# Position products of a self-attention block: eight array tiles of 64 rows and 32 columns for four of 128 rows and 64 columns

## The chip, the cores and the metric

The kernel runs on one core of a Trainium2 chip. A core has TensorE (matrix products, written PE in the profile, with its weight loads as PEld), VectorE (DVE), ScalarE (ACT), GpSimd (POOL) and SyncE (SP), and DMA engines that move data between DRAM and the on-chip memory. Products arrive in PSUM, from which ScalarE or VectorE read them. The metric is the device time in microseconds of one execution: 2402.37 us, the median of three runs (2398.63 to 2405.48). The profiled execution took 2397.5 us.

## The reference

Two bottleneck layers on 16 images of 1024 channels and 32 x 32 pixels, all in fp32. The first has local self-attention over a 3 x 3 window, with 32 heads of 8 channels; the second is an ordinary bottleneck with a 3 x 3 convolution. Cut to what matters here:

```python
q = relu(bn(conv1x1(x, wq)))                    # 256 channels: 32 heads of 8
k = relu(bn(conv1x1(x, wk)))
v = bn(conv1x1(x, wv))
pos = (pos_h + pos_w).reshape(1, c, 9, 1, 1)    # one value per channel and tap
kp = (unfold3x3(k) + pos).reshape(b, HEADS, 8, 9, h, w)
attn = softmax(einsum('bgdhw,bgdkhw->bgkhw', q, kp), axis=taps)
out = einsum('bgdkhw,bgkhw->bgdhw', unfold3x3(v), attn)
```

The logits split into q times the unfolded k, and q times `pos`. The second part is a product over the 8 channels of a head that is the same for every pixel, so TensorE can do it with a block matrix. Because the softmax ignores what all nine taps share, and `pos` is a sum of a part by row and a part by column, four values per head and pixel are enough (`NPOS = 4`: two row offsets and two column offsets against the third). These are the position products: 32 heads x 4 = 128 values for each of 1024 pixels of an image.

## The kernel before

The work is cut into stages by a list in the source: for each image a first 1x1 convolution (C), the projections q and k with the position products (Q), the projection v (V); then a fused stage (F) of the layer's last convolution and the next layer's first one; for each four images a 3x3 convolution in Winograd form (W); and the last 1x1 convolutions (U). The order of all instructions on each engine is written out ahead of time, in the schedule mode where the program's order is kept. A planner, the class `Side`, decides where VectorE's work (attention of an image, transforms for Winograd) is put among the TensorE stages; it counts with fixed costs, and the change does not touch those. The program builds the same sequence on TensorE, VectorE and ScalarE before and after, but for the position products.

`project(b)` makes q, k and v of one image. Its parts come in this order: k of the first 128 channels, q of both halves of the channels, k of the second 128 channels, then `positions()`, then v of both halves. Each convolution takes a tile of PSUM (`ps`, four in all, each of 1024 columns, which is two banks of 512), and ScalarE takes it out again: `norm` at L481 writes q, or writes k and v into `kp`, a padded buffer in the on-chip memory that k and v share. From `kp` each half goes to DRAM through SyncE's queue (L493), so v of a half may be written only once the store of k from there has landed.

`positions()` multiplies `pos`, a table of 128 channels by 64 columns for each half `n` of the channels (16 heads x 4 offsets, and zeros where the channel is not of the head), with q. It makes four matmuls: for each half of the pixels (512 columns) and each `n`, all 128 channels in, 64 values out. The output of `n` = 0 is on partitions 0 to 63 of `ps`, of `n` = 1 on 64 to 127. Seen from the array, these are two column tiles, each of 128 rows and 64 columns. ScalarE copies `ps` into `by_offset` (L515), and two DMAs on GpSimd's queue (L520) store it to DRAM in the order that attention wants: `by_quarter` gives a room of [quarter of the pixels, `n`, 64 values, 256 pixels]. From there it comes back as `pc` (L561), and VectorE adds it to the logits (L602, L605).

`by_offset` has one of three buffers in `zpool`, which transforms and Winograd results on VectorE and ScalarE share. GpSimd's queue is in order, and carries also the stores of q (L526), the loads for attention (L561) and most loads of inputs and stores of results (L345, L433). `fetch_attended` and `finish_attended` (L676 to L693) bring an attended image back from DRAM and apply a ReLU on ScalarE (L690) before the fused stage uses it (L405). VectorE's exp step is two ScalarE instructions (L628), which have a fixed place in ScalarE's order.

Of the kernel before, what the change touches and what calls it, by code (L numbers as in the profile page):

```python
# [13 lines left out]
P = 128  # L14
# [4 lines left out]
NW = WID // P  # L19
# [7 lines left out]
NJ = 4  # L27
JROWS = H // NJ
JPIX = JROWS * W
PW = W + 2  # L30
HALO = (JROWS + 2) * PW
NPOS = 4
FIRST = 4
G = P // HEAD_DIM
# [38 lines left out]
def sa_bottleneck_kernel(ctx: ExitStack, tc: tile.TileContext, x, w1t, wqkvt, w3t, u1t, u2t, u3t, params, out):  # L73
    nc = tc.nc
# [59 lines left out]
    def done_with(key):  # L134

        if last_use[key] == now[0]:
            more_weights()
# [3 lines left out]
    def col(name, j, n=1):  # L141
        return par[:, _COL[name] + j : _COL[name] + j + n]
# [42 lines left out]
    pos = const.tile([P, NW, G, NPOS], F32, tag="pos", name="pos")  # L185
# [117 lines left out]
    def inside(t, n):  # L303
        return t[:, n, 1 : 1 + H, 1 : 1 + W]

    def rows(ap):
        return ap.rearrange("p (r w) -> p r w", w=W)

    def halves(half):
        return slice(half * HALF, (half + 1) * HALF)  # L310
# [53 lines left out]
    def piece(name, half):  # L364
        return name, owner[now[0], name, half], half
# [87 lines left out]
    def by_quarter(name, b, width, per):  # L453


        t = dram.tile([NJ, NW, P * per // HEAD_DIM, width], F32, tag=f"{name}{b}", name=name)
        return t.rearrange("j n c w -> n c j w"), t.rearrange("j n (g d) w -> (j n g) (d w)", d=per)

    def project(b):

        h = hidden.pop(b)

        def conv(which, n):
            ps = psum.tile([P, HW], F32, tag="ps", name="ps")
            name, at = ("wqk", which * WID) if which < 2 else ("wv", 0)
            key, at = piece(name, 0), at + n * P
            for m in range(NW):
                for half in range(2):
                    nc.tensor.matmul(  # L469
                        ps[:, halves(half)],  # L470
                        pieces[key][:, m, at : at + P],
                        h[:, m, halves(half)],
                        start=(m == 0),
                        stop=(m == NW - 1),
                    )
            if n == NW - 1 and which:
                done_with(key)
            return ps

        def norm(dst, src, name, n, func):  # L480
            nc.scalar.activation(  # L481
                dst, src, func,
                bias=col(f"L0_conv_{name}_b", n), scale=col(f"L0_conv_{name}_s", n),
            )

        def halo(name, which, func):

            room, backs[name] = by_quarter(name, b, HALO, HEAD_DIM)
            for n in range(NW):
                norm(inside(kp, n), rows(conv(which, n)), name, n, func)  # L490

                block = kp[:, n]
                nc.sync.dma_start(  # L493
                    room[n], AP(block.tensor, block.offset, [block.ap[0], [JROWS * PW, NJ], [1, HALO]])
                )
                yield CHUNK

        backs = relaid[b] = {}
        q = hpool.tile([P, NW, HW], F32, tag="h", name=f"q_{b}")
        room, backs["q"] = by_quarter("q", b, JPIX, HEAD_DIM)  # L500

        def positions():

            ps = psum.tile([P, HW], F32, tag="ps", name="ps")
            for half in range(2):
                for n in range(NW):
                    nc.tensor.matmul(  # L507
                        ps[n * G * NPOS : (n + 1) * G * NPOS, halves(half)],
                        pos[:, n].rearrange("p g t -> p (g t)"),
                        q[:, n, halves(half)],  # L510
                        start=True,
                        stop=True,
                    )
            by_offset = zpool.tile([P, HW], F32, tag="z", name="by_offset")
            nc.scalar.activation(by_offset, ps, AF.Identity)  # L515

            room, backs["pos"] = by_quarter("pos", b, JPIX, NPOS)
            by_offset = by_offset.rearrange("p (j w) -> p j w", j=NJ)
            for n in range(NW):
                nc.gpsimd.dma_start(room[n], by_offset[n * G * NPOS : (n + 1) * G * NPOS])  # L520

        k = halo("bnk", 1, RELU)
        yield next(k)
        for n in range(NW):
            norm(q[:, n, :], conv(0, n), "bnq", n, RELU)
            nc.gpsimd.dma_start(room[n], q[:, n, :].rearrange("p (j w) -> p j w", j=NJ))  # L526
            yield CHUNK
        yield next(k)
        positions()
        side.add(b)  # L530
        written.add(("qk", b))
        relay("qk", b)
        yield 2.5
        for n, cost in enumerate(halo("bnv", 2, AF.Identity)):
            if n:
                written.add(("v", b))
                relay("v", b)
            yield cost
# [11 lines left out]
    def relay(what, b):  # L550

        if not ((what, b) in written and (what, b) in room_for):
            return
        moved, backs = projected.setdefault(b, {}), relaid[b]
        if what == "qk":
            shapes = (("q", "qc", [HEAD_DIM, JPIX]), ("bnk", "bnk", [HEAD_DIM, HALO]), ("pos", "pc", [NPOS, JPIX]))
        else:
            shapes = (("bnv", "bnv", [HEAD_DIM, HALO]),)
        def move(name, tag, shape):
            t = apool.tile([P] + shape, F32, tag=tag, name=f"{tag}_{b}")  # L560
            nc.gpsimd.dma_start(t.rearrange("p d w -> p (d w)"), backs[name])  # L561
            moved[name] = t.rearrange("p d (r w) -> p d r w", w=PW) if shape[1] == HALO else t
            if len(moved) in (3, 4):
                come[what, b] = max(side.vector, side.tensor) if b else side.tensor

        for i, shape in enumerate(shapes):
            if b < 2 or i == 0:
                move(*shape)
            else:

                moves.append((side.tensor + GAP * i, lambda shape=shape: move(*shape)))
# [841 lines left out]
```

## Time and profile before

| | busy us | share of 2397.5 us | instructions |
|---|---|---|---|
| PE matmuls | 2365.3 | 99% | 6112 |
| PE weight loads | 1143.9 | 48% | 6112 |
| VectorE | 2163.7 | 90% | 1783 |
| ScalarE | 935.0 | 39% | 891 |
| GpSimd | 465.8 | 19% | 853 |

The position matmuls are 128 records (two for each fp32 matmul, four matmuls for each of 16 images), from 50.0 to 1907.6 us. Their first starts lie near 50, 103, 153, 203, 311, 422, 472, 577, 682, 822, 1174, 1224, 1364, 1607, 1766 and 1906 us. The copy at L515 runs 16 times at 1.02 us, the stores at L520 32 times with 0.63 us of issue each, and land 6.4 us later in the median.

In the profile a line such as `L507 PE MATMUL ps<-q,pos` names the source line, the engine, the operation and what it writes and reads. A wait line names who waited and for what, then the us in all, the number of waits and the longest. In a timeline the first number is the start in us, the second the time until the last of the merged instructions ended, and brackets hold the idle time before it and what ended it. An engine that is busy 99% may still run below its peak, since matmuls overlap; how far apart they start says more than how long one lasts.

### The profile page before, as it was taken

To read this page: it belongs to the slowest core of one execution; us is meant where nothing else is said; L and a number is where in the kernel's file an instruction comes from. 1 tells how busy PE (TensorE), PEld (TensorE's weight loads), DVE (VectorE), ACT (ScalarE), POOL (GpSimd) and SP (SyncE) were. 2 spreads that over 40 slices of the span, in tenths; PEclk is the share of its full clock that TensorE was granted. 3 is DMA by queue.
4 is the path that set the end of the run, shared out by engine and by line. 5 is a ranking of instruction groups with operands and counts; after the bars stand their busy time and mean duration, and the time that the engine had idled before them with its cause. 6 is when DMAs were issued, how large, how long until landed. Compare 5 with 4: busy or idle time off the path is not lost.

```text
span 2397.5 us, 18521 instructions
## 1 busy us (share of the span) xinstructions
PE 2365.3 (99%) x6112; PEld 1143.9 (48%) x6112; DVE 2163.7 (90%) x1783; ACT 935.0 (39%) x891; POOL 465.8 (19%) x853
## 2 busy tenths in 40 slices
PE   8999999999999999999999999999999999999998
PEld 3444444444466444444466444444466444444843
DVE  4799998999999999998999999999989999875687
ACT  3323242233222574433122574334222553344278
POOL 3111111111111232111111232111111221111222
PEclk9999999999999999999999999999999999999999
DMA  9969686887798998686888998688788896788977
GB/s 358 350 229 313 241 280 227 258 302 250 287 318 264 322 394 317 225 265 222 260 308 290 306 396 304 233 277 282 251 301 301 308 353 223 255 281 268 331 285 294
DMA packets 295999, 691.05 MB, mean 288 GB/s; under 512 B 20064, under 2 KB 166496, under 8 KB 287456
## 3 DMA queue, kind: packets, MB, share of 16 engines
q0 software_dynamic: 118880, 470.87, 54.4%
q1 hardware_dynamic: 175648, 214.49, 28.3%
q10 hardware_dynamic: 1376, 4.51, 0.5%
q8 instruction: 49, 0.80, 0.1%
q14 instruction: 46, 0.38, 0.0%
HBM read 416.09 MB, written 273.70 MB: 288 GB/s over the span
## 4 chain that ended last, share of the span: by engine, by line
PE 92%; DVE 3%; DMA 3%; ACT 1%; issue 1%; ACTq 0%; SPq 0%; DVEq 0%
PE ps L373 36%; PE ps L405 29%; PE ps L469 13%; PE ps L786 9%; PE ps L1219 4%; PE ps L507 1%; DVE acc L646 1%; DVE acc L664 1%; DMA a<-a 1%; DMA bnk<-kp 1%; DMA U<-uw 0%; DMA uw<-u 0%; DMA V__2_8221<-v 0%; DMA v<-v 0%; DVE form L715 0%
## 5 line engine op out<-in xcount | busy, mean ns | idle before, releaser
L405 PE MATMUL ps<-a,w 128*128 128x512 f32 x1024 | 459.6, 594 | 4.3 <-ACT a L690 4.3
L373 PE MATMUL ps<-result,u 128*128 128x512 f32 x1024 | 459.8, 594 | 3.8 <-ACT result L432 3.8
L373 PE MATMUL ps<-x,w 128*128 128x512 f32 x1024 | 444.4, 595 | 6.4 <-DMA x<-in_x_dram 6.4
L646 DVE TENSOR_TENSOR acc<-e,bnv 128x2048 f32<-128x2048 f32 x144 | 327.6, 2283 | 33.6 <-ACT e L628 30.5
L405 PE MATMUL ps<-y,u 128*128 128x512 f32 x768 | 331.1, 592 | 0.0
L589 DVE TENSOR_TENSOR prod<-qc,bnk 128x2048 f32<-128x2048 f32 x144 | 324.0, 2287 | 1.7
L432 ACT ACTIVATE result<-ps,par 128x1024 f32<-128x1024 f32 x128 | 142.6, 1114 | 463.8 <-PE ps L405 395.4
L373 PEld LDWEIGHTS ps<-x,w 128*128 128x128 f32 x1024 | 195.4, 191 | 252.1 <-issue 251.9
L405 PEld LDWEIGHTS ps<-a,w 128*128 128x128 f32 x1024 | 194.8, 191 | 251.2 <-issue 242.5
L373 PEld LDWEIGHTS ps<-result,u 128*128 128x128 f32 x1024 | 194.8, 190 | 250.7 <-issue 238.2
L664 DVE TENSOR_TENSOR acc<-acc 128x2048 f32<-128x2048 f32 x128 | 293.4, 2292 | 4.4
L405 PEld LDWEIGHTS ps<-y,u 128*128 128x128 f32 x768 | 145.9, 190 | 183.3 <-issue 181.5
L469 PE MATMUL ps<-h,wqk 128*128 128x512 f32 x512 | 222.3, 592 | 0.0
L433 POOL DMA_DIRECT2D r<-result x128 | 68.8, 538 | 633.4 <-ACT result L432 618.0
L594 DVE TENSOR_TENSOR prod<-prod 128x2048 f32<-128x2048 f32 (+1 forms) x80 | 166.2, 2078 | 2.5
L469 PEld LDWEIGHTS ps<-h,wqk 128*128 128x128 f32 x512 | 97.2, 190 | 122.6 <-issue 110.0
L1052 ACT ACTIVATE h<-ps,par 128x1024 f32<-128x1024 f32 x32 | 38.6, 1205 | 280.6 <-PE ps L373 280.6
L432 ACT ACTIVATE result<-ps,bn_sh 128x1024 f32<-128x1024 f32 x96 | 106.6, 1112 | 102.5 <-PE ps L405 102.1
L481 ACT ACTIVATE kp<-ps,par 128x1024 f32<-128x1024 f32 x64 | 77.4, 1210 | 156.5 <-PE ps L469 114.6
L396 ACT ACTIVATE ps<-s 128x1024 f32<-128x1024 f32 x128 | 131.2, 1025 | 2.5
L345 POOL DMA_DIRECT2D x<-in_x_dram x120 | 63.8, 532 | 300.5 <-PE ps L373 229.3
L809 ACT ACTIVATE z<-ps 128x1024 f32<-128x1024 f32 x48 | 49.2, 1025 | 178.1 <-PE ps L786 130.4
(375 smaller groups left out, 2671.4 us busy)
## 6 DMA issues: line engine op xcount, KB each, us to landing
s<-in_x_dram POOLq DMA_DIRECT2D x128, 512.0 KB, 6.2
r<-result POOLq DMA_DIRECT2D x128, 512.0 KB, 4.1
out_dram<-result POOLq DMA_DIRECT2D x126, 512.0 KB, 6.4
x<-in_x_dram POOLq DMA_DIRECT2D x120, 512.0 KB, 5.1
r<-r POOLq DMA_DIRECT2D x111, 512.0 KB, 7.1
v<-v SPq DMA_DIRECT2D x96, 408.0 KB, 4.9
U<-uw SPq DMA_DIRECT2D x72, 512.0 KB, 4.1
bnk<-kp SPq DMA_DIRECT2D x32, 680.0 KB, 7.4
```

What stands on the lines that cost most here:

```text
L373: nc.tensor.matmul(ps[n][:, halves(half)], wt[:, c % (NC // 2), n * P : (n + 1) * P], src[:, halves(half)], start=(c == first), stop=(c == ...
L396: nc.scalar.activation(ps, loaded.pop((self.kind, self.b, o)), AF.Identity)
L405: nc.tensor.matmul(self.ahead[o][:, halves(half)], pieces[key][:, n, o % (NC // 2) * P :][:, :P], self.src[:, n, halves(half)], start=Fals ...
L432: nc.scalar.activation(to_, ps, RELU, bias=self.shift(o), scale=1.0)
L469: nc.tensor.matmul(ps[:, halves(half)], pieces[key][:, m, at : at + P], h[:, m, halves(half)], start=(m == 0), stop=(m == NW - 1),)
L481: nc.scalar.activation(dst, src, func, bias=col(f"L0_conv_{name}_b", n), scale=col(f"L0_conv_{name}_s", n),)
L589: nc.vector.tensor_tensor(by_row(t[:, two]), by_row(qc), kc[:, :, i : i + JROWS, j : j + W], ALU.mult)
L594: nc.vector.tensor_add(u[:, :, 0:4], u[:, :, 0:4], u[:, :, 4:8])
L646: nc.vector.tensor_tensor(by_row(dst), rows(e[:, k, :]).unsqueeze(1).to_broadcast([P, HEAD_DIM, JROWS, W]), vc[:, :, i : i + JROWS, j : j ...
L664: nc.vector.tensor_add(acc, acc, t)
L786: nc.tensor.matmul(acc[i][:, at, :, n, :], pieces[key][:, m, at, n * P : (n + 1) * P], v[:, at, :, m * (TILES + TR) :][:, :, :TILES], star ...
L1219: nc.tensor.matmul(ps, w, by, start=i in (1, 2, 7) and not (i == 2 and self.end), stop=True, skip_group_check=True)
```

## The change

Each position matmul is cut in two along the rows. The 16 heads of a half `n` belong to 128 channels; heads 0 to 7 use only channels 0 to 63, heads 8 to 15 only channels 64 to 127, and the rest of `pos` is zeros. So a matmul of 64 rows (channels) and 32 columns (8 heads x 4) holds all that is not zero. There are eight of them, for two row halves, two halves of the pixels and two `n`. `quadrant` chooses the 32 partitions of the output so that each of the eight has an array tile of its own, and so that two tiles that share columns of the array write different banks of PSUM. The aim is that all eight run at once in the array, in the place of two at once.

The price is that the outputs of the second half of the pixels lie in another order of partitions: the two groups of 32 in each `n` are swapped. The copy out of PSUM stays one instruction. The stores become five: one of 128 partitions for the first half of the pixels, whose order is the natural one, and four of 32 partitions for the second.

```diff
-            for half in range(2):
-                for n in range(NW):
-                    nc.tensor.matmul(
-                        ps[n * G * NPOS : (n + 1) * G * NPOS, halves(half)],
-                        pos[:, n].rearrange("p g t -> p (g t)"),
-                        q[:, n, halves(half)],
-                        start=True,
-                        stop=True,
-                    )
+
+            def quadrant(n, row, half):
+                return (2 * n + (row ^ half)) * P // 4
+
+            for row in range(2):
+                part, heads = slice(row * P // 2, (row + 1) * P // 2), slice(row * G // 2, (row + 1) * G // 2)
+                for half in range(2):
+                    for n in range(NW):
+                        to = quadrant(n, row, half)
+                        nc.tensor.matmul(
+                            ps[to : to + P // 4, halves(half)],
+                            pos[part, n, heads].rearrange("p g t -> p (g t)"),
+                            q[part, n, halves(half)],
+                            start=True,
+                            stop=True,
+                        )
             by_offset = zpool.tile([P, HW], F32, tag="z", name="by_offset")
             nc.scalar.activation(by_offset, ps, AF.Identity)
...
+            nc.gpsimd.dma_start(
+                AP(room.tensor, room.offset, [[JPIX, P], [P * JPIX, NJ // 2], [1, JPIX]]), by_offset[:, : NJ // 2]
+            )
             for n in range(NW):
-                nc.gpsimd.dma_start(room[n], by_offset[n * G * NPOS : (n + 1) * G * NPOS])
+                for row in range(2):
+                    at = quadrant(n, row, 1)
+                    nc.gpsimd.dma_start(
+                        room[n][row * P // 4 :][: P // 4, NJ // 2 :], by_offset[at : at + P // 4, NJ // 2 :]
+                    )
```

## The prediction

> **What bounds the kernel now.** I read the busy times first, then the waits of TensorE, then the order in time round one position product, then the chain of waits.
>
> ```profile
> PE 2365.3 (99%) x6112; PEld 1143.9 (48%) x6112; DVE 2163.7 (90%) x1783; ACT 935.0 (39%) x891; POOL 465.8 (19%) x853
> ...
> PE ps L405 <- ACT a L690: 4.3, 2, 2.9
> PE ps L373 <- ACT result L432: 3.8, 1, 3.8
> ...
> PE ps L469 <- ACT by_offset L515: 2.2, 1, 2.2
> ```
>
> TensorE (PE) is busy 99% of 2397.5 us, and its waits (us in all, times, longest) are single events: one at the start, one at 208 us (L469), one at 326 us (L373, for a result), the rest near the end (L405, for the attended image 15). Between 331 and 2121 us it never waits. So TensorE time taken out there comes off the end, unless VectorE (DVE, 90%) is so close behind that it becomes the bound.
>
> The timelines of the weight loads and of the matmuls near 311 us (image 4) show what a position product costs (start, duration, engine, line):
>
> ```profile
> 310.40 0.59 PE L469 MATMUL ps<-h,wqk 128*128 128x512 f32 x1
> 310.92 0.65 PE L507 MATMUL ps<-q,pos 128*64 128x512 f32 x2
> ...
> 310.92 0.20 PEld L507 LDWEIGHTS ps<-q,pos 128*64 128x64 f32 x4 [0.76 <-issue]
> 311.40 0.14 PEld L507 LDWEIGHTS ps<-q,pos 128*64 128x64 f32 x2 [0.29 <-issue]
> 311.83 0.14 PEld L507 LDWEIGHTS ps<-q,pos 128*64 128x64 f32 x2 [0.29 <-issue]
> 312.79 0.30 PEld L469 LDWEIGHTS ps<-h,wv 128*128 128x128 f32 x2 [0.81 <-issue]
> 313.32 0.19 PEld L469 LDWEIGHTS ps<-h,wv 128*128 128x128 f32 x1 [0.24 <-issue]
> 313.75 0.19 PEld L469 LDWEIGHTS ps<-h,wv 128*128 128x128 f32 x1 [0.24 <-issue]
> ```
>
> Each fp32 matmul of the program is two records, two passes. Full-width passes start 0.43 us apart (313.32, 313.75). The eight records of the four position matmuls start in pairs, at 310.92, 311.40, 311.83 and 312.3: the two column tiles already run beside each other. From the last full-width start before (310.40) to the first regular one after (313.32) is 2.92 us; without the block it would be 2 x 0.43 = 0.86. The block costs 2.06 us: four slots of 0.43 (1.72), and 0.34 at its two ends, where the array changes its tiling.
>
> **What the Trainium skill says.** "TensorEngine Tiling (Array Packing)", section Key Properties: different tiles load weights and multiply in parallel, and a change of tiling mode drains TensorE. The trace agrees on both: the pairs above, and the 0.34 us. "TensorE: Matmul & The Clock Gate", section Part 3, gives 10.6 times for 16 tiles of 32 x 32 and a span of one matmul plus about 4 ns for each further tile; the trace has only two tiles at once, and no row tiles. "PSUM — Partial Sum Buffer", section on bank collisions, says that row tiles must not write one bank and quadrant at once; here the XOR in `quadrant` sends the two row halves of one column strip to different banks. Nothing in the trace tests it.
>
> **The change, part by part.**
>
> *Matmuls.* Four of 128 rows and 64 columns go, eight of 64 rows and 32 columns come, still 512 columns of q each, so a pass should still take 0.43 us. Each of the eight has a tile of its own. If all start together, the block has two slots (first and second passes): 0.86 + 0.34 + 7 x 0.004 (the page's price of a tile, an estimate) = 1.23 us. Saved: 0.83 us an image. Upper bound 0.86 (no stagger), lower bound 0.72, if the first load and change cost a further 0.1. Sixteen images give 13.3 us at most.
>
> *Where it is lost.* Images 0 to 3 come before the wait at 208 us. Two lines of the chain there, after which TensorE goes on at 210.81:
>
> ```profile
> 208.67 1.19 ACT kp L481
> 209.85 0.91 ACT by_offset L515
> ```
>
> ScalarE reads image 3's positions at 209.85 because it stood at L690 until 207.5, waiting for the attended image 0 (a<-a), which VectorE ended at 189 and DMA brought. None of this hangs on TensorE; TensorE would come 4 x 0.83 = 3.3 us earlier and wait 3.3 us longer. Image 4 comes before the wait at 326 us, which ends with a kp store issued at 316.01 behind VectorE's v stores on the same queue and landing 12.23 us later; VectorE had no wait on TensorE there, so I count 0.83 as lost too. Images 5 to 15 (position products at 422 to 1906 us) keep theirs: 11 x 0.83 = 9.1 us.
>
> *Whether VectorE keeps up.* Only the attention of image 15 is late in the chain. Its waits on TensorE, through ScalarE's order, are its reserve (start, duration, wait before it):
>
> ```profile
> 1128.42 2.29 DVE L646 TENSOR_TENSOR acc<-e,bnv 128x2048 f32<-128x2048 f32 x1 [10.09 <-ACT e L628]
> ...
> 1780.16 1.23 DVE L816 TENSOR_TENSOR z<-z 128x1024 f32<-128x1024 f32 x1 [4.93 <-ACT z L809]
> ...
> 2062.78 4.49 DVE L646 TENSOR_TENSOR acc<-e,bnv 128x2048 f32<-128x2048 f32 x2 [8.71 <-ACT e L628]
> ```
>
> An exp wait can't fall under 2.1 us (two ScalarE exps; others in the trace are that long). With the 4.56 us of another exp wait at 1646 us, 8.0 + 2.5 + 4.9 + 6.6 = 22 us of reserve lie before image 15's last accumulation, against 9.1 needed; 14 of them after 1640. Image 15's chain (VectorE to 2109, two DMAs, ReLU at 2127.9) then moves with TensorE, and so do the last Winograd stage and the tail.
>
> *Weight loads.* 16 records an image for 8, of 32 columns rather than 64 (0.14 us each now). They lie beside matmuls; only the first is on the path, and that is in the 0.34.
>
> *Stores.* Two issues on GpSimd's queue become five. The trace has 0.63 us for an issue of 64 x 4 runs, 0.53 for 128 x 1 and 0.77 for 128 x 4, so 0.63 for 128 x 2 and at most 0.53 for each 32 x 2: 2.75 for 1.26 us, +1.5 us an image. GpSimd is busy 19%, and sits 4.36 us waiting for by_offset before them. Queued behind them are the loads of later tiles (q, k, positions, the next inputs); in a Winograd stage GpSimd waited 1.33 us for TensorE after them, so the first load behind is late by 1.5 + 0.83 - 1.33 = 1.0 us against TensorE, with its user over 10 us away. Bytes and 1 KB runs are the same. Cost: nothing.
>
> *The buffer.* by_offset is freed when the last of five stores lands, up to 1.5 us after the second did, less the 0.83. VectorE waited for that buffer once, 1.2 us, in the whole run. At most a few us in sum, out of its reserve.
>
> *ScalarE.* The copy out of PSUM (1.02 us) is unchanged, and its wait for the products (8.5 us in 13 times) mostly goes; ScalarE is 39% busy.
>
> Sum: 2402.4 - 9.1 = 2393.3 us.
>
> **The rivals.**
>
> 1. *All sixteen images count.* If contention eases and the store and attended tile at 326 and 208 us come earlier: 2402.4 - 13.3 = 2389. Against it: those waits hang on VectorE and DMA. Chance 0.10.
>
> 2. *A new wait eats part.* TensorE comes 0.83 us sooner to every wait for a kp store (ScalarE already waits 41.9 us in 11 times for bnk<-kp), or the longer hold of by_offset delays VectorE. Half the gain: 2398. Chance 0.12.
>
> 3. *Row halves take turns*, because both feed the same column strips: two rounds of two slots, the block stays at 1.72 + 0.34, plus a few ns: 2402 to 2403. Chance 0.13.
>
> 4. *The second passes block the queue.* In program order both passes of a matmul precede the next matmul. If TensorE overtakes only as far as it shows now, pairs remain: eight slots, 3.43 + 0.34, +1.72 us for 11 images = +19 us: 2421, slower. If one waiting pass may be overtaken at a time, five slots, +0.43 each: 2407. Against it speaks image 0, where three matmuls had waited for q's second half and then started together:
>
> ```profile
> 52.70 0.20 PEld L507 LDWEIGHTS ps<-q,pos 128*64 128x64 f32 x4 [2.50 <-ACT q L481]
> 53.18 0.14 PEld L507 LDWEIGHTS ps<-q,pos 128*64 128x64 f32 x1 [0.29 <-issue]
> 53.61 0.14 PEld L507 LDWEIGHTS ps<-q,pos 128*64 128x64 f32 x1 [0.29 <-issue]
> ```
>
> Four loads at once are both passes of two matmuls, on different tiles; the later one had passed the earlier one's second pass. The third shared its tile and had to follow. That is overtaking by tile, but it shows only one step. Chance 0.15.
>
> **How the numbers follow.** The forecast has 0.50 and is the likeliest: 2393.3. The bounds of its term (0.72 to 0.86) give 2392.9 to 2394.5, and the runs before spread by 3.8 us below and 3.1 above their median. The range 2387 to 2407 takes in this case, rivals 1 to 3 and the mild form of 4, and leaves out the eight slots. The limits of 0.3% are 2395.2 and 2409.6. Faster: 0.43 of the forecast's 0.50, all of rival 1, 0.02 of rival 2: 0.55. Slower: nearly all of rival 4's eight slots and strays of the mild one: 0.13. The rest, 0.32, is no change.
>
> **What would show it.** Right, if the position block has two groups of starts 0.48 us apart and the next full-width start comes 1.05 us after the first, not 1.87; if TensorE's waits at 208 and 326 us are longer by 3.3 and 0.8 us; if the exp wait at 2062 us shrinks. Wrong, if the starts come in more than two groups, if TensorE waits for kp stores or positions at new places, or if image 15's attended tile comes no earlier.

## The result, and the profile after

The changed kernel took 2394.26 us in the median (2392.73 to 2396.15) against 2400.72 us of the kernel before: a ratio of 0.9965, 95% interval 0.9949 to 0.9982. The medians are 6.5 us apart; the ratio on record means 8.4 us (4.3 to 12.3). A second comparison with more runs gave 0.9976 (0.9968 to 0.9984), that is 5.8 us (3.8 to 7.7). The forecast was 9.1 us less: inside the first interval, outside the narrower second one.

The block in the array does what was foreseen. Busy times of the page, then the timeline round image 1's products, first of the weight loads, then of the matmuls (start, us, engine, line):

```profile
PE 2357.5 (98%) x6240; PEld 1141.1 (48%) x6240; DVE 2163.4 (90%) x1783; ACT 933.2 (39%) x891; POOL 490.8 (20%) x901
```

```profile
102.63 0.18 PEld L514 LDWEIGHTS ps<-q,pos 64*32 64x32 f32 x16 [0.76 <-issue]
103.65 0.30 PEld L469 LDWEIGHTS ps<-h,wv 128*128 128x128 f32 x2 [0.84 <-issue]
...
102.63 1.09 PE L514 MATMUL ps<-q,pos 64*32 64x512 f32 x16
103.65 0.70 PE L469 MATMUL ps<-h,wv 128*128 128x512 f32 x1
```

All sixteen weight loads are done within 0.18 us, before the first pass is over. The next full-width start comes 1.02 us after the first of the block, where it was 1.87. In the trace the eight first passes start 6.6 ns apart (the prediction took 4), the second passes 0.45 us after the first. The block costs 1.22 us for 2.07, so 0.85 us an image. Each image has it but image 0, where the products wait for q and 0.5 us is saved.

That is 13.3 us of TensorE time, and about half of it arrives. TensorE's waits in the changed kernel (us in all, times, longest) say where it stands now:

```profile
PE ps L405 <- ACT a L704: 5.5, 2, 3.5
PE ps L469 <- ACT by_offset L522: 4.2, 1, 4.2
PE ps L800 <- ACT z L823: 3.5, 3, 1.7
PE ps L405 <- ACT ps L396: 2.3, 2, 1.2
```

The first two were there before (4.3 and 2.2 us; in a second profile of before 5.8 and 1.9). The last two are new: waits in the Winograd stages (L800) and, at 833 and 1936 us, for a seed of PSUM (L396). Gone is the wait at 326 us.

The length of a wait isn't all that it costs. The profile also records the clock that was granted to TensorE (PEclk, 1.00 is full). Here are the 8 us round the wait at 208 us, in the second profile of before and then in the change, with the eight matmuls that follow the wait:

```profile
core 0: us, PE busy (x) PEld busy (x) DVE busy (x) ACT busy (x) POOL busy (x), PEclk, DMA share, GB/s
208.00:216.00 8.00, 6.12 (x15) 2.58 (x14) 7.86 (x6) 5.39 (x6) 2.19 (x4) 1.00 1.06 349
208.00:216.00 8.00, 5.90 (x7) 2.52 (x8) 7.86 (x5) 5.08 (x6) 3.98 (x7) 0.58 1.07 338
```

```profile
210.40 3.70 PE L469 MATMUL ps<-h,wv 128*128 128x512 f32 x8 [1.88 <-ACT by_offset L515]
210.10 6.65 PE L469 MATMUL ps<-h,wv 128*128 128x512 f32 x8 [4.18 <-ACT by_offset L522]
```

In the change the clock stood at half for 6.8 us from 209.2 us on, and the same eight matmuls, most of them now 0.86 us apart where they were 0.43, took 6.65 us for 3.70. So a wait that is 2.3 us longer cost 5.3 us. The table below has this in it: what TensorE loses at a place is the wait and the half clock after it.

A comparison of starts of the same instructions in two traces shows the course of it. The base is a second profile of the kernel before, of 2402.46 us, since the first one was its fastest run. Lead over it in us, each trace counted from its first matmul (a minus is behind):

| place, us | TensorE | VectorE | what happens next |
|---|---|---|---|
| 199 | 2.8 | 1.1 | wait for attended image 0 |
| 213 | -2.5 | 1.1 | wait for the kp store of image 4 |
| 350 | 6.0 | 2.6 | |
| 680 | 9.4 | 8.3 | first Winograd stage |
| 717 | 6.4 | 6.4 | |
| 819 | 7.2 | 6.4 | kp store of image 9 |
| 900 | 5.8 | 5.8 | |
| 1221 | 7.5 | 5.9 | second Winograd stage |
| 1240 | 6.2 | 5.9 | |
| 1903 | 9.4 | 8.2 | kp store of image 15 |
| 1950 | 8.2 | 8.2 | attention of image 15 |
| 2126 | 6.6 | 7.7 | |
| end | 6.5 | 6.5 | |

TensorE gains 0.85 us with each product and gives its lead back where it meets VectorE or a store. After the meetings at 680, 819 and 1903 us and at the end the two leads are equal to a tenth: the two engines go in step. That neither alone sets the time is for the experiments to show. The reserve of VectorE isn't used: its exp wait near the end is as long as before (before: 8.71).

```profile
2055.89 4.49 DVE L660 TENSOR_TENSOR acc<-e,bnv 128x2048 f32<-128x2048 f32 x2 [8.69 <-ACT e L642]
```

The first new wait in the Winograd stage, timeline of the changed kernel:

```profile
689.55 1.02 ACT L823 ACTIVATE z<-ps 128x1024 f32<-128x1024 f32 x1 [5.51 <-DMA pos<-by_offset]
690.61 1.23 DVE L830 TENSOR_TENSOR z<-z 128x1024 f32<-128x1024 f32 x1 [2.06 <-ACT z L823]
690.63 3.72 PE L800 MATMUL ps<-V__2_2452,U 128*128 128x256 f32 x16 [0.75 <-ACT z L823]
...
717.03 3.72 PE L800 MATMUL ps<-V__2_2644,U 128*128 128x256 f32 x16 [1.71 <-ACT z L823]
```

ScalarE can't take the third Winograd sum out of PSUM, since the buffer it wants is by_offset's, whose stores have not landed. That is the hold of a buffer which I had costed at "a few us in sum, out of its reserve". The first theory after the result was therefore:

- **Theory 1**: the missing part goes to the five stores, through the hold of by_offset's buffer.
- **Theory 2**: it goes to VectorE, which can't follow; the stores don't matter.

### The profile page after: what moved, and what is told of

It is laid out like the page before. It is cut to its first block, busy times and chain, and to the rows that moved or that the text cites. A ratio compares the mean times of both kernels' runs of the same rounds, so it can differ in the third digit from the quotient of the medians.

```text
span 2394.4 us, 18854 instructions
## 1 busy us (share of the span) xinstructions
PE 2357.5 (98%) x6240; PEld 1141.1 (48%) x6240; DVE 2163.4 (90%) x1783; ACT 933.2 (39%) x891; POOL 490.8 (20%) x901
## 5 line engine op out<-in xcount | busy, mean ns | idle before, releaser
L660 DVE TENSOR_TENSOR acc<-e,bnv 128x2048 f32<-128x2048 f32 x144 | 327.6, 2284 | 31.7 <-ACT e L642 28.6
L481 ACT ACTIVATE kp<-ps,par 128x1024 f32<-128x1024 f32 x64 | 77.4, 1210 | 154.9 <-PE ps L469 113.1
L396 ACT ACTIVATE ps<-s 128x1024 f32<-128x1024 f32 x128 | 131.2, 1025 | 2.5
L469 PE MATMUL ps<-h,wv 128*128 128x512 f32 x256 | 117.0, 610 | 4.2 <-ACT by_offset L522 4.2
```

The source lines that it names most:

```text
L396: nc.scalar.activation(ps, loaded.pop((self.kind, self.b, o)), AF.Identity)
L469: nc.tensor.matmul(ps[:, halves(half)], pieces[key][:, m, at : at + P], h[:, m, halves(half)], start=(m == 0), stop=(m == NW - 1),)
L481: nc.scalar.activation(dst, src, func, bias=col(f"L0_conv_{name}_b", n), scale=col(f"L0_conv_{name}_s", n),)
L660: nc.vector.tensor_tensor(by_row(dst), rows(e[:, k, :]).unsqueeze(1).to_broadcast([P, HEAD_DIM, JROWS, W]), vc[:, :, i : i + JROWS, j : j ...
```

## The experiments

Figures are microseconds against runs of the kernel before that were taken beside each kernel, worked out as the ratio less one, times 2402, with the 95% interval. Waits and clocks are of one profiled execution of each kernel; those of e9, e1 and e13 were 7, 5 and 4 us above their medians.

| run | edit | against before | interval |
|---|---|---|---|
| after_again | the change | -5.8 | -7.7 to -3.8 |
| e1 | eight tiles, two stores | -2.4 | -4.3 to -0.7 |
| e2 | the change, second half in a buffer of its own | -6.0 | -8.6 to -3.6 |
| e3 | four tiles, five stores | -2.2 | -4.6 to +0.2 |
| e4 | the change from image 4 on | -2.6 | -4.3 to -1.2 |
| e6 | no position products | -1.9 | -4.1 to +0.2 |
| e9 | the change, kp stored from ScalarE's queue | +5.3 | +2.9 to +7.4 |
| e10 | before, kp stored from ScalarE's queue | +15.1 | +12.0 to +18.0 |
| e11 | before, less VectorE work | -9.6 | -12.5 to -7.0 |
| e12 | the change, less VectorE work | -19.9 | -22.8 to -17.1 |
| e13 | e1 with three small copies | -6.0 | -9.6 to -2.4 |

### The stores: after_again, e1, e2, e3

> The changed kernel once more, beside the kernel before on the chip of the other three runs. Every theory: 6 to 7 us under the kernel before, the position block 0.85 us shorter in each of 16 images. It is the base that the other three are held against.

> The eight tiles, but two stores of 64 partitions as before. The second half of the pixels is thus stored with its groups of 32 partitions swapped, and the logits get wrong offsets there; the work is otherwise the same. Theory 1 (part of the gain is lost because five stores hold the buffer of by_offset longer, and in the Winograd stages the third copy out of PSUM waits for that buffer): the waits of ScalarE for DMA pos<-by_offset go from 11.9 us to under 3, TensorE's 2.7 and 1.2 us losses in the stages at 690 and 1237 us go, and the time is 2 to 4 us under the changed kernel, some 9 to 10 under the kernel before. Theory 2 (what is lost is lost because VectorE can't keep up, and the stores don't matter): within 1 us of the changed kernel.

```diff
-            nc.gpsimd.dma_start(
-                AP(room.tensor, room.offset, [[JPIX, P], [P * JPIX, NJ // 2], [1, JPIX]]), by_offset[:, : NJ // 2]
-            )
             for n in range(NW):
-                for row in range(2):
...
+                nc.gpsimd.dma_start(room[n], by_offset[n * G * NPOS : (n + 1) * G * NPOS])
```

> The changed kernel with the second half of the pixels copied into a buffer of its own (2 KB a partition, not shared with the Winograd copies), the first half into the shared one; two ScalarE copies of 512 columns for one of 1024. The shared buffer is then held for one store, not five. Theory 1: as e1_two_stores, 2 to 4 us under the changed kernel, though five stores remain. Theory 2: within 1 us of the changed kernel, or above it by the second copy (16 times 0.2 us on ScalarE, mostly hidden).

```diff
-            by_offset = zpool.tile([P, HW], F32, tag="z", name="by_offset")
-            nc.scalar.activation(by_offset, ps, AF.Identity)
...
+            one = zpool.tile([P, HW], F32, tag="z", name="by_offset")[:, :HALF]
+            two = opool.tile([P, HALF], F32, tag="o", name="offset_two")
+            nc.scalar.activation(one, ps[:, :HALF], AF.Identity)
+            nc.scalar.activation(two, ps[:, HALF:], AF.Identity)
...
```

> The kernel before with its stores alone cut into five (128 partitions for the first half of the pixels, four times 32 for the second), in the natural order; the matmuls are those of before. It gives the price of the stores without the gain. Theory 1: 0 to 3 us above the kernel before, with ScalarE waits for DMA pos<-by_offset in the Winograd stages. Theory 2: within 1 us of the kernel before. If the stores cost GpSimd's queue more than I counted (its work behind them is late), 4 us or more above.

```diff
             for n in range(NW):
-                nc.gpsimd.dma_start(room[n], by_offset[n * G * NPOS : (n + 1) * G * NPOS])
+                for row in range(2):
+                    at = (2 * n + row) * P // 4
+                    nc.gpsimd.dma_start(
+                        room[n][row * P // 4 :][: P // 4, NJ // 2 :], by_offset[at : at + P // 4, NJ // 2 :]
+                    )
```

(Ahead of that loop e3 has the store of 128 partitions of the change.)

Theory 1 falls as an account of the time. In e2 the waits of ScalarE for by_offset's stores are gone from the list (11.9 us in the change), and the time is the same. At its place the hold was real: in e2's profile TensorE goes through the first Winograd stage with its lead of 7 us unchanged. But it loses 4.5 us at the next meeting, the kp store of image 9 (2.6 us of waiting, 1.7 by half clock), and both engines leave it with a lead near 3.3. e1, with two stores, missed both theories: it isn't faster than the change but slower, -2.4 against -5.8, with intervals that touch only between -4.3 and -3.8. Five stores with the old matmuls cost nothing that shows (e3). So the added stores seem to help. In which way? ScalarE's waits for the kp stores (L481), first in e1, then in the change:

```profile
ACT kp L481 <- DMA bnk<-kp: 51.0, 12, 9.4
```

```profile
ACT kp L481 <- DMA bnk<-kp: 35.3, 8, 7.1
```

In the profiles with three more issues on GpSimd's queue in every image (the change in both profiles, e2, e3, e13) this sum is 35.3, 37.0, 38.3, 35.9 and 38.7 us; in those with two stores (before in both profiles, e1, e6) it is 41.9, 40.7, 51.0 and 52.3. e4, with five stores from image 4 on, has 41.7. It is largest where TensorE comes early and the stores are two. The largest single wait is that at 326 us. SyncE's and GpSimd's queues there, in the second profile of before and then in the change:

```profile
313.50 1.26 POOL L520 DMA_DIRECT2D pos<-by_offset  x2 [4.36 <-ACT by_offset L515]
...
315.18 2.11 SPq L131 DMA_DIRECT2D w<-ws  x1
...
317.38 1.71 SPq L493 DMA_DIRECT2D bnk<-kp  x1
...
329.52 1.21 ACT L481 ACTIVATE kp<-ps,par 128x1024 f32<-128x1024 f32 x1 [11.09 <-DMA bnk<-kp]
```

```profile
314.30 0.60 SPq L131 DMA_DIRECT2D w<-ws  x1
315.00 1.09 SPq L493 DMA_DIRECT2D bnk<-kp  x1
315.33 0.71 POOL L526 DMA_DIRECT2D pos<-by_offset  x1 [3.58 <-ACT by_offset L522]
...
325.11 1.21 ACT L481 ACTIVATE kp<-ps,par 128x1024 f32<-128x1024 f32 x1 [4.85 <-DMA bnk<-kp]
```

Here the kp store is issued 2.4 us earlier, and ScalarE gets on 10 us after it rather than 12. That the kp store goes ahead of the position stores can't be the reason: in the second profile of the change it goes behind their start (314.89 after 313.60 us), and the stall is still short. What sets the two groups apart is the weight load (L131) ahead of the kp store on SyncE's queue. It took 0.60 us to issue in all five profiles with three more issues, and 1.9 to 2.1 us in three of the four with two stores. Why, no run shows. TensorE's stall at this place was 3.8 and 5.7 us in the two profiles of before, 4.1 in e1, 3.8 in e3 and 7.0 in e6; it is none and 2.4 in the two of the change, 0.6 in e2, 2.2 in e13, 1.2 in e4. So five stores alone don't shorten it (e3). Of the few us by which e1 falls short, a part is seen at this wait, and a part at the next kp store, where TensorE waits 3.4 us at 839 us for 1.2 and 2.3 in the change.

### Which engine binds: e4, e6, e11, e12

> The change for images 4 to 15 alone; images 0 to 3 keep the matmuls and stores of before. Prediction's step: the first four save nothing at the end, because TensorE waits at 208 us for the attended image 0, which VectorE and DMA bring. If so, the time is that of the changed kernel, ratio 0.997 to 0.998 to the kernel before, and TensorE's wait at 208 us is back near 2.3 us. If the four count: 3.4 us above the changed kernel, ratio about 0.999.

```diff
-            ps = psum.tile([P, HW], F32, tag="ps", name="ps")
+            if b >= 4:
+                ps = psum.tile([P, HW], F32, tag="ps", name="ps")
...
+            else:
+                ps = psum.tile([P, HW], F32, tag="ps", name="ps")
...
```

> The kernel before without the position products at all: by_offset is copied from q, so the logits get wrong offsets; copy and two stores stay. It takes 2.07 us of TensorE off each image, 33 us in all, and asks how much of such time reaches the end. If TensorE alone binds after the first five images (the prediction): 11 times 2.07, 23 us under the kernel before, 2380. If VectorE, the kp stores and the attended tiles are next in line (theory K, after the runs so far: less than half of 13.6 us arrived): 12 to 16 us under. If VectorE binds at once: under 8.

```diff
-            ps = psum.tile([P, HW], F32, tag="ps", name="ps")
...
-            nc.scalar.activation(by_offset, ps, AF.Identity)
+            nc.scalar.activation(by_offset, q[:, 1], AF.Identity)
```

> The kernel before without the last of eight accumulating adds of the attention on VectorE (2.3 us an image, 37 us in all; the ninth tap is so left out of the result). Taking all position products off TensorE (33 us) gave 2 us. Theory V (VectorE is as much the bound as TensorE, and TensorE falls back to it at the fused and Winograd stages): this gives more than that, 6 to 14 us under the kernel before, then TensorE binds. Theory P (TensorE alone binds, and the product-free run lost its gain elsewhere): under 3 us.

```diff
-            nc.vector.tensor_add(acc, acc, t)
+            if k < KK - 1:
+                nc.vector.tensor_add(acc, acc, t)
```

> The changed kernel with the same add left out. Held against e11_less_vector it gives what the eight tiles are worth where VectorE is out of the way. Theory V: 9 to 13 us under e11 (0.85 us for each of 11 to 16 images), against 5.7 us between the two kernels with all of VectorE's work. Theory P: the same 5 to 6 us.

The edit of e12 is that of e11, in the changed kernel.

e6 is the most telling run. All 33 us of the products are gone from TensorE, and the time falls by 1.9 us, or not at all. (It also takes one tile of PSUM an image out of the rotation, so TensorE's time is not all that changes.) Part of what takes their place stands in TensorE's waits in e6:

```profile
PE ps L776 <- DMA U<-uw: 7.4, 3, 5.0
PE ps L405 <- ACT ps L396: 7.2, 3, 2.5
PE ps L373 <- ACT result L432: 7.0, 1, 7.0
...
PE ps L469 <- ACT kp L481: 5.2, 1, 5.2
PE ps L469 <- ACT h L1042: 3.9, 1, 3.9
PE ps L776 <- ACT z L799: 3.6, 1, 3.6
```

All of TensorE's waits in this list add up to 48.4 us in e6 and to 25.7 in the second profile of before. That is 23 of the 33 us. The other 10 are in the clock: TensorE's busy time is only 22.9 us less, because it worked at half clock eight times after waits, where before did three times. Both profiles have a span of 2400.8 us. Of the outcomes on record for e6 only the last, "VectorE binds at once: under 8", takes the measured time in.

The same account for the other kernels, in us. The half clock's cost is taken as half of TensorE's busy time in the stretches in which the clock stood at half; the last column is the difference of the two profiled spans.

| | product time taken out | more waits of TensorE | more cost of half clock | left | spans |
|---|---|---|---|---|---|
| the change against before | 13.3 | 2.9 | 3.3 | 7.1 | 6.4 |
| e6 against before | 33.1 | 22.9 | 9.9 | 0.3 | 0.0 |
| e11 against before | 0 | -8.1 | -1.7 | 9.8 | 10.0 |
| e12 against e11 | 13.3 | 2.1 | 1.1 | 10.1 | 10.9 |

These are single profiles, but the clock that each run lists goes the same way: its mean is 0.992 over the 13 runs of e6 and 0.996 over the runs of before beside it, 0.998 over those of e11 and 0.997 beside it.

e11 takes 37 us off VectorE and gains 9.6, more than TensorE's 33 us gave, and the account says where: TensorE waits less, and is less often at half clock. With VectorE lighter, the eight tiles are worth their price: e12 is 9.7 us under e11 (medians 2381.59 and 2391.32), against 5.8 with all of VectorE's work, and near the 9.1 of the forecast. In e11 VectorE waits more where it was held back before, for its exps (28.6 us in the change, 30.5 in before):

```profile
DVE acc L646 <- ACT e L628: 59.6, 11, 12.6
```

This supports theory V: both engines bind, in turn. VectorE's part need not be its own pace alone. Its stores stand on SyncE's queue with the kp stores, and ScalarE's waits for those fall to 16.7 us in e11 and 14.6 in e12; no run keeps VectorE's work and moves its stores alone.

e4 went against my step that images 0 to 3 save nothing: it is at -2.6, where the change is at -5.8, and the intervals hardly overlap. Yet both profiles of the change show the lead of TensorE gone at 208 us. What the first four give may lie with the stores, or in VectorE's start, which was 1.1 and 0.7 us earlier by then in the two profiles of the change. In e4's profile TensorE loses more at the first Winograd stage, from a lead of 7.1 us to 2.4. No run tells these apart; it stays open.

### The kp stores: e9, e10, e13

> The changed kernel with the stores of kp issued from ScalarE's queue, right behind the instruction that writes kp, and no longer from SyncE's, where they stand behind VectorE's v stores and weight loads. It shortens the wait of the next v norm for that store. Theory K (TensorE comes earlier to the v projection and then waits for ScalarE, which stands at the landing of the kp store): ScalarE's waits for DMA bnk<-kp fall from 35 to 51 us to under 25, TensorE's stalls at 326 and 831 us go, and the time is 3 to 6 us under the changed kernel. If those stores are slow because the DMA engines are full, not because of their queue: within 1 us, or above it by ScalarE's issue time (64 times 0.36 us at most).

```diff
-                nc.sync.dma_start(
+                nc.scalar.dma_start(
                     room[n], AP(block.tensor, block.offset, [block.ap[0], [JROWS * PW, NJ], [1, HALO]])
                 )
```

> The kernel before with the same move of the kp stores to ScalarE's queue. With e9 it shows what the eight tiles are worth once that wait is shorter. Theory K: 2 to 5 us under the kernel before (the stall at 326 us goes), and e9 is 8 to 10 us under this one, more than the 5.7 us that the change gives without it. If the wait isn't what takes the gain: e9 is 5 to 6 us under this one.

The edit of e10 is the same, in the kernel before.

The waits for the kp stores fall as meant, to 21.3 us in e9 and 20.3 in e10, and yet both kernels are slower. VectorE pays: it waits longer for its own v stores, and for the position stores that free a buffer for them. From VectorE's waits in e10 (in the second profile of before 12.1 and 1.5 us):

```profile
DVE v L715 <- DMA v<-v: 18.8, 6, 7.7
...
DVE v L715 <- DMA pos<-by_offset: 7.0, 1, 7.0
```

The v stores as a whole don't land later (4.6 us in the median from issue to landing, 4.9 in the second profile of before); single ones do, where VectorE waits for them. Past the wait at 326 us VectorE is 7 us later than in the first profile of before, by 600 us 12 us, while TensorE is still only 2 us later. So the wait was real, but to shorten it at VectorE's cost is a loss: one more sign that VectorE binds too. Between these two kernels, the eight tiles give 9.8 us (2408.12 against 2417.90), as theory K had it, though its main claim, that both become faster, fell.

> e1_two_stores (eight tiles, two stores, the second half's groups swapped) with three small extra copies of 2 KB behind the stores on GpSimd's queue. They delay what stands behind by as much as the three added stores do, some 1.6 us, without cutting the stores. With two stores the eight tiles gave 2.4 us, with five 5.7. Theory D (what helps is that the loads behind on GpSimd's queue start later, out of the way of the kp store): near 5.7 us under the kernel before, ScalarE's waits for bnk<-kp near 36 us. Theory G (what helps is the finer cut of the stores): near 2.4 us, waits near 51 us.

```diff
                 nc.gpsimd.dma_start(room[n], by_offset[n * G * NPOS : (n + 1) * G * NPOS])
+            for i in range(3):
+                small = dram.tile([P // 4, G], F32, tag=f"small{b}_{i}", name="small")
+                nc.gpsimd.dma_start(small, members[: P // 4])
```

e13 comes to -6.0, and its waits for kp are 38.7 us for e1's 51.0: theory D, delay of what stands behind on GpSimd's queue, fits, and a finer cut of the stores isn't needed for it. The interval (-9.6 to -2.4, from seven runs) still overlaps that of e1, and what the delay changes on SyncE's queue isn't known, so this is favoured, not settled.

> The kernel before once more, for a second profile of it: the first one is of its fastest run (2398.6 us). Every theory: near 2402 us, and the same waits of TensorE at 208, 326 and after 2110 us, shifted by DMA's scatter.

It took 2402.46 us. Its waits at 208 and 326 us are 1.9 and 5.7 us, and it is the base of the table of leads above.

## Why the prediction was right, and where not

- **The matmuls.** Right, nearly to the digit: 0.85 us an image where I took 0.83; two groups of starts, 0.45 us apart for 0.48 foretold; the next full-width start at 1.02 us for 1.05. Rivals 3 and 4 are out: row halves don't take turns, and TensorE overtakes second passes of seven other matmuls.
- **The wait at 208 us.** TensorE's lead is lost there as foretold, but not in the way foretold. The wait grew from 1.9 or 2.2 to 4.2 us, not by 3.3, and the half clock after it took another 3.0 us, for which the prediction has no term. e4 says that the first four images are worth about 3 us in the end. So the step that counts them as lost fails by e4, in a way that stays open.
- **The wait at 326 us.** Wrong: it didn't grow by 0.8 us, it went from 3.8 and 5.7 us in the two profiles of before to none and 2.4 in those of the change. I had read that the kp store hangs on VectorE's queue, and not asked what else would change its time of issue.
- **VectorE keeps up.** This step failed. I summed 22 us of VectorE's reserve, nearly all after 1120 us, and asked only about image 15. But TensorE meets VectorE in each Winograd stage and ScalarE at each kp store before that. At the first stage VectorE's reserve was the 2.33 us of its wait at 695.7 us, which I had left out, and TensorE lost 3.0 us there. At 832, 1238 and 1937 us it lost 1.5, 1.3 and 1.2 us. The 1.7 at image 15 are of another kind: its waits there are no longer than in the second profile of before (5.5 and 5.8 us), but half clock cost 2.0 us more.
- **Time taken out of TensorE comes off the end, since it never waits.** Wrong as a rule. An engine without a wait is in step with others that may have little slack; e6 took out 33 us and got 1.9.
- **A wait costs its length.** The prediction took this for granted. In the change 3.3 of the 13.3 us went to more half clock after waits, in e6 9.9 of 33.
- **The stores cost nothing.** Right in sum, and more than that: with two stores the change gives 2.4 us, with five 5.8. The wait for by_offset's buffer was 11.9 us on ScalarE, more than the few us that I allowed, and it did hold TensorE in the Winograd stages; but taking it away (e2) gave nothing in the end, since the lead was lost at the next kp store.
- **The sum.** 9.1 foretold; 8.4 by the first comparison, 5.8 by the larger one. The right sign and nearly the right size came in part by luck, from two errors against each other: a gain of several us at 326 us that I had not seen, and losses of nearly 9 us from 690 us on. The mechanism is more that of rival 2, a new wait that eats part. Of the prediction's own signs, the two groups of starts came true. But TensorE waited at new places, and the exp wait near the end didn't shrink (8.69 us for 8.71). Where VectorE is lighter (e12) the sum comes out near what I had.

## What to carry to other kernels

Where two engines are busy 90% or more, take the work of each away in turn in a trial before tuning either: here 33 us off TensorE gave 1.9 us and 37 us off VectorE gave 9.6, though TensorE showed 99% busy and hardly a wait. Ask for the reserve of the other engine at each place where the two meet, not for its sum. Look at the granted clock after each wait of TensorE, for a longer wait can cost about twice what it adds: here 2.3 us more of waiting cost 5.3. And an edit's transfers may matter by when they go and not only by what they move: look for the store that someone waits for, and for what stands ahead of it.

## What the runs showed of the hardware

- Eight array tiles of 64 rows and 32 columns ran eight fp32 products of 512 columns in one block of 1.22 us: two groups of passes 0.45 us apart, tiles started 6.6 ns apart. Row tiles wrote one bank of PSUM at once in different groups of 32 partitions.
- Going into the smaller tiling and out again cost about 0.36 us (1.22 less two passes of 0.43), the same with eight tiles as with two.
- Besides the one at each run's very end, the 14 profiles have 55 stretches of half clock, of 3.4, 6.8 or 10.2 us. Before each, by 1.6 to 5.3 us, a wait of TensorE of at least 1.5 us had begun. No shorter wait stood alone before one, and some longer ones had none (3.8 us at 326 us in e3). In such a stretch full-width passes started 0.86 us apart.
- A DMA of 32 partitions cost GpSimd 0.54 us of issue, one of 128 with two runs each 0.71; cutting two stores into five cost 1.6 us of its time an image and, in e3, no time at the end.
- With the kp stores issued from another queue (e9, e10), VectorE waited up to 9.4 and 7.7 us for a v store of its own, where 3.4 us was the longest in before at that line.
